# Experts on their chosen rows only: sorted blocks of 128 rows in place of dense experts

## The chip, the cores and the metric

The kernel runs on one core of a Trainium2 chip. Five engines work side by side, each with its own instruction queue in a fixed order: TensorE (PE, matmuls, with PEld for the loading of its weights), VectorE (DVE), ScalarE (ACT), GpSimd (POOL) and SyncE (SP, which mainly issues DMAs). ACT and POOL can issue DMAs too. An instruction that waits holds back all that stand behind it in its engine's queue. The metric is the device time of one execution in microseconds (us), lower is better. All numbers are float32.

## The reference, cut to what matters

x is 16 sequences of 256 tokens with 128 features. Attention has 16 heads of width 8, causal; then a feed-forward part with 8 experts of which each token uses its two best, and two layer norms.

```python
x = _layernorm(x + attention(x))              # w_qkv, rotary positions, causal softmax, w_proj
flat_x = x.reshape(-1, 128)                   # 4096 rows
logits = flat_x @ W_router + b_router         # 8 experts
top_vals, top_idx = top_k(logits, 2)
router_weights = softmax(logits where chosen, -inf elsewhere)
for e in range(8):
    h = relu(flat_x @ W1[e] + b1[e])          # 128 -> 512
    y = h @ W2[e] + b2[e]                     # 512 -> 128
    final_output += y * (router_weights[:, e] * chosen[:, e])[:, None]
x = _layernorm(x + final_output)
```

The weight of an expert that a token did not choose is zero, so only two of the eight products per token count.

## The kernel before

Tokens go in tiles of 128 rows; a sequence has two tiles (NT), a feed-forward block has two sequences (BB), so four tiles or 512 tokens. All weights of all experts are loaded once and stay on the chip (`w1_sb`, `w2_sb`, lines 103 to 107), with DMAs issued by SP.

`attention(b, x1)` is a generator that yields after each step. It transposes the sequence (line 170), makes Q and K (lines 179 and 182, 128x256 matmuls), V (202), and then goes through 12 units. A unit is one bank of scores: `scores` does one matmul with 32 rows of contraction, as four heads of width 8 share a row group (222), DVE adds the causal mask and takes the maximum (230, 232), ACT the exponentials (237); two units later `turn` transposes four 128x128 pieces on PE (246) and copies them back (249 on ACT, 251 on DVE); one unit later `weigh` does eight (four for the first query tile) matmuls with only 9 columns (262). `finish` divides, transposes (279), multiplies by w_proj (284), adds the residual (286) and normalizes: statistics on DVE (146, 147), the root on POOL (149, 150), the result on DVE (152).

`experts(blk, x1)` is a second generator. It transposes the block's 512 rows (314), does the router (321 and small DVE operations) and then all eight experts on all 512 rows: four 128x512 matmuls per expert into `ps_h` (391), relu and bias on ACT (394), sixteen 128x128 matmuls into `ps_y` (401) and on DVE the weighted sum into `acc` (411). Then the second layer norm, and a DMA to the output.

The loop at lines 428 to 448 runs the experts of one block in between the attention steps of the next: for 44 attention steps 39 expert steps are taken. So the attention of the first two sequences runs without expert work beside it, and the experts of the last block without attention. The tile framework then orders each engine's instructions by priority and puts in all waits. It keeps DMAs of the SP and ACT queues on eight semaphores in turn, and a DMA waits until the previous one of its semaphore has landed.

In the trace a float32 matmul appears as two records (x512 for 256 matmuls in line 391), a PE transpose as one.

Of the kernel before, what the change touches and what calls it, by code (L numbers as in the profile page):

```python
# [11 lines left out]
F32 = mybir.dt.float32  # L12
AF = mybir.ActivationFunctionType
ALU = mybir.AluOpType
AX = mybir.AxisListType
PSUM = bass.MemoryType.PSUM

P = 128  # partitions, and the model's width
HEADS = 16
HD = 8  # width of a head  # L20
GROUPS = 4  # row groups of the tensor engine, four heads in each
# [5 lines left out]
def kernel(  # L27
# [16 lines left out]
    nc = tc.nc  # L44

    B, S, D = x.shape
    E, _, FF = w1.shape
    NT = S // P  # token tiles of a sequence
    FC = FF // P
    BB = 2  # sequences of a feed-forward block  # L50
    G = BB * NT  # token tiles of a block
    TB = G * P

# [6 lines left out]
    p4 = ctx.enter_context(tc.tile_pool(name="p4", bufs=4))  # L60
    ps_sc = ctx.enter_context(tc.tile_pool(name="ps_sc", bufs=2, space=PSUM))
# [3 lines left out]
    ps_h = ctx.enter_context(tc.tile_pool(name="ps_h", bufs=2, space=PSUM))  # L65
    ps_y = ctx.enter_context(tc.tile_pool(name="ps_y", bufs=1, space=PSUM))

# [10 lines left out]
    w1_sb = const.tile([P, E, FF], F32, name="w1_sb")  # L78
    w2_sb = const.tile([P, E, FC, D], F32, name="w2_sb")
    b2_sb = const.tile([G * E, G, D], F32, name="b2_sb")  # L80

# [18 lines left out]
    nc.gpsimd.memset(b2_sb, 0.0)  # L100
    for g in range(G):
        nc.sync.dma_start(b2_sb[g * E : (g + 1) * E, g, :], b2)
    for e in range(E):
        nc.sync.dma_start(w1_sb[:, e, :], w1[e])
        nc.sync.dma_start(w2_sb[:, e, :, :], w2[e].rearrange("(c p) d -> p c d", p=P))
        if e + 2 < B:
            load_x(e + 2)
    for b in range(E + 2, B):
        load_x(b)

# [1 line left out]
    ident = const.tile([P, P], F32, name="ident")  # L112
    make_identity(nc, ident)
    # 0 where the key is not after the query, for the diagonal blocks of four heads
# [11 lines left out]
    # E - e, so that of equal logits the first one has the largest  # L126
    rank = const.tile([P, G, E], F32, name="rank")
    for e in range(E):
        nc.gpsimd.memset(rank[:, :, e : e + 1], float(E - e))
    neg_half = const.tile([P, G], F32, name="neg_half")  # L130
    nc.gpsimd.memset(neg_half, -0.5)

    # the weights of Q and K with the halves of each head swapped
# [6 lines left out]

    def normalize(dst, r, n, tag):
        """Rows of r [P, n, D] to mean 0 and variance 1, into dst."""
        mv = p4.tile([P, n, 2], F32, tag=f"mv{tag}", name="mv")
        for t in range(n):
            st = p4.tile([P, 6], F32, tag=f"st{tag}", name="st")
            nc.vector.bn_stats(st, r[:, t, :])
            nc.vector.bn_aggr(mv[:, t, :], st)  # L147
        rstd = p4.tile([P, n], F32, tag=f"rstd{tag}", name="rstd")
        nc.gpsimd.tensor_scalar(rstd, mv[:, :, 1], EPS, None, ALU.add)  # L149
        nc.gpsimd.tensor_tensor(rstd, rstd, neg_half[:, :n], ALU.pow)  # L150
        for t in range(n):
            nc.vector.tensor_scalar(  # L152
                dst[:, t, :],
                r[:, t, :],
                mv[:, t, 0:1],
                rstd[:, t : t + 1],
                ALU.subtract,
                ALU.mult,
            )

# [1 line left out]
    def attention(b, x1):  # L162
# [12 lines left out]
        # Q and K by head on the partitions, turned by their positions  # L175
# [14 lines left out]
        # K four times, each with one head of each row group and zeros elsewhere  # L190
# [6 lines left out]
        # V by token, with a column of ones after each head  # L197
# [14 lines left out]
        # units: (query tile, row group, its heads), one bank of scores each  # L212
# [98 lines left out]
    def experts(blk, x1):  # L311
        psx = ps_misc.tile([P, TB], F32, tag="misc", name="ps_x1T")
        for g in range(G):
            nc.tensor.transpose(psx[:, ts(g, P)], x1[:, g, :], ident)
        x1T = p2.tile([P, TB], F32, tag="x1T", name="x1T")
        nc.scalar.copy(x1T, psx)  # L316
        yield

        psl = ps_misc.tile([P, G, E], F32, tag="misc", name="ps_lg")
        for g in range(G):  # L320
            nc.tensor.matmul(  # L321
                psl[:, g, :], x1T[:, ts(g, P)], wr_sb, start=True, stop=True
            )

        def small(name, last=E):
            return p2.tile([P, G, last], F32, tag=name, name=name)

        def wide(t):
            return t.to_broadcast([P, G, E])

        V = nc.vector
        lg = small("lg")
        for g in range(G):
            V.tensor_tensor(lg[:, g, :], psl[:, g, :], br_sb, ALU.add)

        def first_max(v, tag):
            """The largest of v, and 1 at the first place that has it, 0 elsewhere."""
# [4 lines left out]
            V.tensor_tensor(key, key, rank, ALU.mult)  # L342
# [7 lines left out]
        _, hot2 = first_max(rest, "2")  # L350
        V.tensor_tensor(hot1, hot1, hot2, ALU.add)
        ex = small("ex")
        V.tensor_tensor(ex, lg, wide(m1), ALU.subtract)
        nc.scalar.activation(ex, ex, AF.Exp)
        V.tensor_tensor(ex, ex, hot1, ALU.mult)
        total = small("total", 1)
        V.tensor_reduce(total, ex, AX.X, ALU.add)
        V.reciprocal(total, total)
        wt = small("wt")
        V.tensor_tensor(wt, ex, wide(total), ALU.mult)  # L360
        yield

        acc = p2.tile([P, G, D], F32, tag="acc", name="acc")
        psy = None

        def output_biases():
            """acc = x1 + the experts' second biases, weighted."""
            psw = ps_misc.tile([G * E, P], F32, tag="misc", name="ps_wT")
            nc.tensor.matmul(
                psw, wt.rearrange("p g e -> p (g e)"), ident, start=True, stop=True  # L370
            )
            wT = p2.tile([G * E, P], F32, tag="wT", name="wT")
            nc.scalar.copy(wT, psw)
            yield
            psb = ps_misc.tile([P, G, D], F32, tag="misc", name="ps_b2")
            nc.tensor.matmul(psb, wT, b2_sb, start=True, stop=True)  # L376
            V.tensor_tensor(acc, psb, x1, ALU.add)
            yield

        biases = output_biases()  # L380
        hidden = {}
        for e in range(E + 1):
            if e < E:
                hT = p2.tile([P, FC, TB], F32, tag="hT", name="hT")
                hidden[e] = hT
            if e > 0:
                psy = ps_y.tile([P, G, D], F32, tag="y", name="ps_y")
            for c in range(max(FC, G)):
                if e < E and c < FC:
                    psh = ps_h.tile([P, TB], F32, tag="h", name="ps_h")  # L390
                    nc.tensor.matmul(  # L391
                        psh, w1_sb[:, e, ts(c, P)], x1T, start=True, stop=True
                    )
                    nc.scalar.activation(  # L394
                        hidden[e][:, c, :], psh, AF.Relu, bias=b1_sb[:, e, c : c + 1]
                    )
                if e == 0 and c > 0:
                    next(biases, None)
                if e > 0 and c < G:
                    for f in range(FC):  # L400
                        nc.tensor.matmul(  # L401
                            psy[:, c, :],
                            hidden[e - 1][:, f, ts(c, P)],
                            w2_sb[:, e - 1, f, :],
                            start=(f == 0),
                            stop=(f == FC - 1),
                        )
                yield
            if e > 0:
                for g in range(G):  # L410
                    V.scalar_tensor_tensor(  # L411
                        acc[:, g, :],
                        psy[:, g, :],
                        wt[:, g, e - 1 : e],
                        acc[:, g, :],
# [3 lines left out]
        y = p2.tile([P, G, D], F32, tag="yout", name="yout")  # L419
        normalize(y, acc, G, "f")  # L420
        nc.sync.dma_start(out_t[:, blk * G : (blk + 1) * G, :], y)
        yield
# [3 lines left out]
    ATT_STEPS, FFN_STEPS = 44, 39  # L426
    before = None
    for blk in range(B // BB + 1):
# [78 lines left out]
```

## Time and profile before

| | us |
|---|---|
| median of 3 runs | 1158.97 |
| the runs | 1155.66 to 1171.31 |
| span of the profiled execution | 1160.2 |

The busy time of the main groups, from the page's part 5:

| line | what | busy us | mean ns of a record |
|---|---|---|---|
| 391 | expert matmul 128x512, x512 | 280.4 | 638 |
| 401 | expert matmul 128x128, x2048 | 287.7 | 286 |
| 222 | scores, 32 rows, 512 columns, x384 | 230.6 | 725 |
| 262 | weigh, 9 columns, x1536 | 209.6 | 264 |
| 246 | transposes, x768 | 146.5 | 310 |
| 394 | relu on ACT 128x512, x256 | 176.2 | 688 |

Busy time of PE is a count of the records' extent. A matmul record that lasts longer than the same shape elsewhere is a sign that it ran at another pace, so rows of the same line at two places in the span are worth comparing. The row PEclk of the page shows the granted clock, in tenths of full speed.

### The profile page before, as it was taken

Reading aid. Unit: us, or ns where it says so; the run is one execution under the profiler, and the core shown is the slowest. Engines: PE = TensorE matmul, PEld = TensorE weight load, DVE = VectorE, ACT = ScalarE, POOL = GpSimd, SP = SyncE. Lnnn points to the kernel's source line nnn. Section 1 sums busy time; section 2 is a strip of 40 time slices with the busy share of each in tenths; the row PEclk is TensorE's granted clock in tenths of the full one; section 3 lists DMA queues with packets and bytes.
Section 4 is the critical chain, followed back from the end, with each engine's and each line's share of the span. In section 5 each row is a group of like instructions: output and inputs, shape, how many; then the busy total and the mean of one; then the engine's idle time right before and its main releaser. Section 6 shows DMA issues by size and latency. Waiting matters only on the chain.

```text
span 1160.2 us, 14412 instructions
## 1 busy us (share of the span) xinstructions
PE 1106.2 (95%) x5696; PEld 759.5 (65%) x5696; DVE 523.3 (45%) x1364; ACT 407.8 (35%) x937; POOL 54.4 (5%) x146
## 2 busy tenths in 40 slices
PE   7979899998999999998999989999999989999996
PEld 3656667665676757666676756767566665766675
DVE  4333353546434463445435464344634545344412
ACT  2212143433334244332334433342433324343242
POOL 1000000001000000001000010000000010000000
PEclk9999989999899999999799998999979998899999
DMA  8000000000000000000000000000000000000000
GB/s 231 18 1 0 1 1 1 1 1 10 1 1 1 1 10 1 1 1 10 1 1 1 1 10 1 1 1 1 10 1 1 1 3 8 1 1 2 10 1 10
DMA packets 19202, 10.20 MB, mean 9 GB/s; under 512 B 5280, under 2 KB 17984, under 8 KB 19136
## 3 DMA queue, kind: packets, MB, share of 16 engines
q1 hardware_dynamic: 18560, 8.96, 2.9%
q8 instruction: 45, 0.74, 0.3%
q10 hardware_dynamic: 576, 0.33, 0.1%
q14 instruction: 21, 0.17, 0.0%
HBM read 7.19 MB, written 2.10 MB: 8 GB/s over the span
## 4 chain that ended last, share of the span: by engine, by line
PE 90%; DVE 6%; POOL 2%; ACT 1%; issue 1%; DMA 0%; POOLq 0%; DVEq 0%; ACTq 0%
PE ps_y L401 21%; PE ps_h L391 19%; PE ps_sc L222 19%; PE ps_av L262 15%; PE ps_tr L246 10%; DVE acc L411 1%; PE ps_proj L284 1%; PE ps_qk L182 1%; PE ps_qk L179 1%; DVE parts L184 1%; POOL rstd L150 1%; PE ps_lg L321 1%; DVE yout L152 1%; DVE nmax L232 1%; PE ps_b L376 1%
## 5 line engine op out<-in xcount | busy, mean ns | idle before, releaser
L401 PEld LDWEIGHTS ps_y<-w_sb,hT 128*128 128x128 f32 x2048 | 275.0, 201 | 99.7 <-issue 85.9
L394 ACT ACTIVATE hT<-ps_h,b_sb 128x512 f32<-128x512 f32 x256 | 176.2, 688 | 405.1 <-PE ps_h L391 405.1
L401 PE MATMUL ps_y<-w_sb,hT 128*128 128x128 f32 x2048 | 287.7, 286 | 3.2 <-DVE acc L411 3.2
L391 PE MATMUL ps_h<-x1T,w_sb 128*128 128x512 f32 x512 | 280.4, 638 | 0.0
L222 PE MATMUL ps_sc<-kTm,qk 32*128 32x512 f32 x384 | 230.6, 725 | 0.8 <-DVE kTm L193 0.8
L237 ACT ACTIVATE pr<-ps_sc,nmax 128x256 f32<-128x256 f32 (+1 forms) x512 | 180.3, 420 | 134.5 <-DVE nmax L232 133.8
L230 DVE TENSOR_TENSOR ps_sc<-ps_sc,causal 128x256 f32<-128x256 f32 (+1 forms) x192 | 99.9, 520 | 277.2 <-PE ps_sc L222 276.8
L262 PEld LDWEIGHTS ps_av<-vaug,pT 128*128 128x128 f32 x1536 | 215.7, 217 | 0.0
L262 PE MATMUL ps_av<-vaug,pT 128*128 128x9 f32 x1536 | 209.6, 264 | 0.0
L246 PEld LDWEIGHTS ps_tr<-ident,pr 128*128 128x128 f32 x768 | 97.2, 155 | 138.8 <-issue 103.1
L246 PE MATMUL ps_tr<-ident,pr 128*128 128x128 f32 x768 | 146.5, 310 | 7.3 <-ACT pr L237 6.8
L411 DVE SCALAR_TENSOR_TENSOR acc<-ps_y,wt,acc 128x128 f32<-128x128 f32 x256 | 76.8, 342 | 156.1 <-PE ps_y L401 156.1
L232 DVE TENSOR_REDUCE nmax<-ps_sc 128x2 f32<-128x512 f32 (+1 forms) x192 | 131.9, 687 | 3.0
L251 DVE COPY pT<-ps_tr 128x512 f32<-128x512 f32 x128 | 88.0, 687 | 38.2 <-PE ps_tr L246 38.2
L391 PEld LDWEIGHTS ps_h<-x1T,w_sb 128*128 128x128 f32 x512 | 83.5, 197 | 30.0 <-issue 19.3
L222 PEld LDWEIGHTS ps_sc<-kTm,qk 32*128 32x128 f32 x384 | 58.8, 203 | 49.0 <-issue 30.9
L249 ACT COPY pT<-ps_tr 128x512 f32<-128x512 f32 x64 | 37.5, 586 | 89.2 <-PE ps_tr L246 89.2
L149 POOL TENSOR_SCALAR rstd<-mv 128x1 f32<-128x1 f32 (+1 forms) x40 | 9.8, 244 | 816.2 <-DVE mv L147 816.2
L184 DVE TENSOR_TENSOR parts<-ps_qk,rope_sb 128x512 f32<-128x512 f32 x32 | 21.9, 685 | 34.0 <-PE ps_qk L182 34.0
L179 PE MATMUL ps_qk<-xT,wqkv_sb 128*128 128x256 f32 x64 | 24.1, 461 | 10.4 <-ACT x1T L316 4.7
L272 DVE RECIPROCAL rec<-ps_av 128x16 f32<-128x16 f32 x32 | 8.2, 258 | 50.8 <-PE ps_av L262 50.1
L150 POOL TENSOR_TENSOR rstd<-rstd,neg_half 128x1 f32<-128x1 f32 (+1 forms) x40 | 26.3, 658 | 3.3
(65 smaller groups left out, 347.4 us busy)
## 6 DMA issues: line engine op xcount, KB each, us to landing
w_sb<-in_L_ffn_W_dram SPq DMA_DIRECT2D x16, 256.0 KB, 5.4
x<-in_L_attn_x_dram SPq DMA_DIRECT2D x16, 128.0 KB, 5.0
out_dram<-yout SPq DMA_DIRECT2D x8, 256.0 KB, 2.3
rope_sb<-in_rope_dram SPq DMA_DIRECT2D x1, 512.0 KB
wqkv_sb<-in_L_attn_w_qkv_dram ACTq DMA_DIRECT2D x1, 192.0 KB, 3.0
wproj_sb<-in_L_attn_w_proj_dram ACTq DMA_DIRECT2D x1, 64.0 KB
bproj_sb<-in_L_attn_b_proj_dram ACTq DMA_DIRECT2D x1, 64.0 KB
b_sb<-in_L_ffn_b_dram SPq DMA_DIRECT2D x4, 4.0 KB
```

The costliest lines, as they stand in the source:

```text
L150: nc.gpsimd.tensor_tensor(rstd, rstd, neg_half[:, :n], ALU.pow)
L222: nc.tensor.matmul(ps, qT[rg, ts(qi, P)], kTm[rg, js[0] : js[0] + len(js), 0:nk], start=True, stop=True,)
L230: nc.vector.tensor_tensor(diag, diag, causal[:, : len(js), :], ALU.add)
L232: nc.vector.tensor_reduce(nmax[:, : len(js)], ps, AX.X, ALU.max, negate=True)
L237: nc.scalar.activation(pr[:, n, :], ps[:, n, :], AF.Exp, bias=nmax[:, n : n + 1])
L246: nc.tensor.transpose(ps[:, n, :], pr[:, ts(n, P)], ident)
L251: nc.vector.tensor_copy(pT, ps)
L262: nc.tensor.matmul(av[qi][:, h, 0 : HD + 1], pT[:, n * (qi + 1) + kt, :], vaug[:, kt, h, :], start=(kt == 0), stop=(kt == qi),)
L391: nc.tensor.matmul(psh, w1_sb[:, e, ts(c, P)], x1T, start=True, stop=True)
L394: nc.scalar.activation(hidden[e][:, c, :], psh, AF.Relu, bias=b1_sb[:, e, c : c + 1])
L401: nc.tensor.matmul(psy[:, c, :], hidden[e - 1][:, f, ts(c, P)], w2_sb[:, e - 1, f, :], start=(f == 0), stop=(f == FC - 1),)
L411: V.scalar_tensor_tensor(acc[:, g, :], psy[:, g, :], wt[:, g, e - 1 : e], acc[:, g, :], ALU.mult, ALU.add,)
```

## The change

Attention stays as it is. The feed-forward part is done anew, in two groups of 8 sequences (16 tiles, 2048 tokens each):

- `logits(b)` follows the attention of each sequence: two transposes of the normalized rows, an ACT copy, two 8-column matmuls, two DVE adds.
- `route(g)`, once per group: the two best experts of each token on DVE, counts by two 128x128 matmuls (a triangle of ones and all ones), a running sum, and from it for each token and choice the row (`dest`) in a table in HBM in which rows are sorted by expert, each expert's run filled up to a multiple of 128. `expert` says for each of the 2*16+8-1 = 39 blocks of 128 rows which expert it belongs to. Then 32 indirect DMAs on the POOL queue write the rows (128 rows of 512 B each) into that table.
- `block(g, j)`, 39 times per group: SP reads the expert's number into a register and loads that expert's parameters (128 x 1156 floats, 592 KB, from a packed copy in HBM) and the block's 64 KB of rows; one transpose, four 128x128 matmuls, a DVE maximum with -b1 in place of relu, four 128x128 matmuls, a DVE add of the bias (b2 plus W2 times b1), a store to a second table issued by ACT.
- `combine(g)`: 32 indirect DMAs on the POOL queue fetch each token's two rows, DVE adds them with their weights, then the layer norm and the store.
- At the start: the packed copy is written from HBM to HBM on the SP queue, zeros are written to the row tables (ten DMAs, 5.1 MB) on the ACT queue, `output_bias` makes the joint bias of each expert with five matmuls.
- The order: group 0's attention without expert work beside it; group 1's attention with group 0's blocks in between; then group 1's blocks and combine.

```diff
+    pack = dram.tile([E, P, WROW], F32, name="pack")
...
     for e in range(E):
-        nc.sync.dma_start(w1_sb[:, e, :], w1[e])
-        nc.sync.dma_start(w2_sb[:, e, :, :], w2[e].rearrange("(c p) d -> p c d", p=P))
+        nc.sync.dma_start(pack[e, :, 0:O2], w1[e])
+        nc.sync.dma_start(
+            pack[e, :, O2:OB].rearrange("p (c d) -> p c d", c=FC),
+            w2[e].rearrange("(c p) d -> p c d", p=P),
+        )
...
+    def output_bias(e):
+        w2_sb = p2.tile([P, FC, D], F32, tag="w2", name="w2_sb")
+        nc.scalar.dma_start(w2_sb, w2[e].rearrange("(c p) d -> p c d", p=P))
...
+            nc.tensor.matmul(
+                ps,
+                b1_sb[:, e, c : c + 1].to_broadcast([P, P]),
+                w2_sb[:, c, :],
...
+        nc.scalar.copy(bias, ps)
+        nc.scalar.dma_start(pack[e, :, OB:ON], bias)
...
+    def logits(b):
+        t0 = b * NT
+        psx = ps_misc.tile([P, S], F32, tag="misc", name="ps_x1T")
+        for t in range(NT):
+            nc.tensor.transpose(psx[:, ts(t, P)], x1_sb[:, t0 + t, :], ident)
+        x1T = p2.tile([P, S], F32, tag="x1T", name="x1T")
+        nc.scalar.copy(x1T, psx)
+        yield
...
+    class Routed:
+        def __init__(self, r, b0, n):
+            self.t0, self.T = b0 * NT, n * NT
+            self.NB = 2 * self.T + E - 1
+            self.rows = dram.tile([self.NB * P, D], F32, tag=f"rows{r}", name="rows")
+            self.back = dram.tile([self.NB * P, D], F32, tag=f"back{r}", name="back")
...
+                nc.scalar.dma_start(flat[:, i : i + n], zeros[:, :n])
...
+        for t in range(T):
+            for k in range(2):
+                put = nc.gpsimd.indirect_dma_start(
+                    out=g.rows[:, :],
+                    out_offset=bass.IndirectOffsetOnAxis(
+                        ap=g.dest[:, k, t : t + 1], axis=0
+                    ),
+                    in_=x1_sb[:, t0 + t, :],
...
+    def block(g, j):
+        e = nc.values_load(
+            g.expert[0:1, j : j + 1],
+            engines=[SP],
...
+        w = p3.tile([P, WROW], F32, tag="w", name="w")
+        nc.sync.dma_start(w, pack[bass.ds(e, 1), :, :].rearrange("o p f -> (o p) f"))
+        rows_in = p3.tile([P, D], F32, tag="rows_in", name="rows_in")
+        nc.sync.dma_start(rows_in, g.rows[ts(j, P), :])
+        yield
+        pst = ps_f.tile([P, P], F32, tag="f", name="ps_rT")
+        nc.tensor.transpose(pst, rows_in, ident)
+        rT = p3.tile([P, P], F32, tag="rT", name="rT")
+        nc.scalar.copy(rT, pst)
+        yield
+        psh = ps_f.tile([P, FC, P], F32, tag="f", name="ps_h")
+        for c in range(FC):
+            nc.tensor.matmul(psh[:, c, :], w[:, ts(c, P)], rT, start=True, stop=True)
...
+        V.tensor_tensor(
+            hT,
+            psh,
+            w[:, ON:WROW].rearrange("p (c o) -> p c o", o=1).to_broadcast([P, FC, P]),
+            ALU.max,
+        )
+        yield
+        psy = ps_f.tile([P, D], F32, tag="f", name="ps_y")
+        for c in range(FC):
...
+        V.tensor_tensor(y, psy, w[:, OB:ON], ALU.add)
+        nc.scalar.dma_start(g.back[ts(j, P), :], y)
+        yield
...
+    def combine(g):
...
+                    nc.gpsimd.indirect_dma_start(
+                        out=yk,
+                        out_offset=None,
+                        in_=g.back[:, :],
...
+        if g.t0 == 0:
+            for i, _ in enumerate(attn):
+                if i % (2 * ATT_STEPS // E * 2) == 0:
+                    next(biases, None)
...
+        else:
+            p = groups[0]
+            left = interleave(attn, n * ATT_STEPS, pending, (p.NB - 6) * FFN_STEPS)
+            pending = left
+        for _ in route(g):
+            next(pending, None)
+            next(pending, None)
+        for _ in pending:
+            pass
+        pending = chain(*(block(g, j) for j in range(g.NB)), combine(g))
+    for _ in pending:
+        pass
```

In the instruction order of the built program, PE has no block in the 8 sequences of group 0, six blocks in each of sequences 8 to 13 (in sequence 8 after the scores of its eighth unit), three in sequence 14, none in sequence 15 and 39 after it. POOL has its 32 writes of group 0 before sequence 8's first normalization, and its fetches of group 0 within sequence 15. On ACT the ten stores of zeros, each of which waits for an earlier DMA, stand ahead of the first sequence's copy of V and of all its exponentials. On PE the two transposes of `logits` stand ahead of the next sequence's first transposes.

More of the change, by code (lines that the diff above doesn't have):

```diff
@@ L16 @@
 PSUM = bass.MemoryType.PSUM
+DRAM = bass.MemoryType.DRAM
+SP = mybir.EngineType.SP
 P = 128
@@ L380, in experts @@
[L380 to L392, printed above, removed]
-                    )
[L394 to L410, printed above, removed]
@@ new lines, in route @@
+        m2, hot2 = first_max(rest, "2")
+        hot = small("hot")
+        V.tensor_tensor(hot, hot1, hot2, ALU.add)
+        psc = ps_misc.tile([P, 2, T, E], F32, tag="misc", name="ps_count")
+        nc.tensor.matmul(psc[:, 0], before, hot, start=True, stop=True)
+        nc.tensor.matmul(psc[:, 1], ones, hot, start=True, stop=True)
+        runs = p2.tile([P, E, T + 1], F32, tag="runs", name="runs")
+        V.tensor_copy(runs[:, :, 0:T], psc[:, 1].rearrange("p t e -> p e t"))
+        total = p2.tile([P, E, 1], F32, tag="total", name="total")
@@ new lines, in route @@
+        V.tensor_tensor(ends, ends, runs, ALU.subtract)
+        place = small("place")
+        V.tensor_tensor(
+            place, psc[:, 0], ends[:, :, 0:T].rearrange("p e t -> p t e"), ALU.add
+        )
+        for k, h in enumerate((hot1, hot2)):
+            V.tensor_tensor(h, h, place, ALU.mult)
+            with nc.allow_low_precision(reason="whole numbers"):
+                V.tensor_reduce(
+                    g.dest[:, k, :].rearrange("p (t o) -> p t o", o=1), h, AX.X, ALU.add
+                )
@@ L418, in experts @@
                     )
[L419 to L428, printed above, removed]
[L429 to L448 removed]
+                yield
```

255 lines of the change are left out of this document (174 added, 81 removed).

## Prediction, made before the changed kernel ran

> **What bounds the kernel now.** I read the page first: busy times and slices.
>
> ```profile
> PE 1106.2 (95%) x5696; PEld 759.5 (65%) x5696; DVE 523.3 (45%) x1364; ACT 407.8 (35%) x937; POOL 54.4 (5%) x146
> PE   7979899998999999998999989999999989999996
> PEclk9999989999899999999799998999979998899999
> ```
>
> PE is busy all the time, and lines 391 and 401, the experts, hold 568 of its 1106 us. That invites the sum "a quarter of the expert work, so 380 us less". Before believing it I cut the span into stretches: sequence 0 from its first scores to those of sequence 1, a steady block, and the last block's experts alone (columns: length, then busy us and count of PE, PEld, DVE, ACT, POOL, granted clock, DMA share, GB/s).
>
> ```profile
> 12.50:77.90 65.40, 59.31 (x188) 39.84 (x188) 25.36 (x52) 14.58 (x42) 2.60 (x7) 1.00 0.30 85
> 431.60:565.10 133.50, 129.47 (x713) 88.85 (x712) 65.17 (x170) 50.64 (x117) 6.53 (x16) 0.97 0.01 3
> 1092.00:1150.00 58.00, 56.78 (x310) 39.27 (x310) 13.24 (x57) 22.25 (x34) 1.27 (x2) 1.00 0.02 5
> ```
>
> One sequence of attention without expert work takes 65.4 us. Two sequences together with a whole block of experts take 133.5 us. So the experts cost almost nothing where they run beside attention, though alone they need some 64 us of PE per block. The rows of single lines say why: the second sequence (77.9 to 134) against a steady stretch (585 to 695), then PE's timeline at one of the places where expert rows are sparse (start, extent in us).
>
> ```profile
> L222 PE MATMUL ps_sc<-kTm,qk x24: 1056/1136/1217, 77.9 to 119.1; 32*128 32x512 f32 x24
> L222 PE MATMUL ps_sc<-kTm,qk x36: 587/640/692, 588.8 to 694.1; 32*128 32x512 f32 x36
> L246 PE MATMUL ps_tr<-ident,pr x48: 421/421/476, 82.0 to 128.5; 128*128 128x128 f32 x48
> L246 PE MATMUL ps_tr<-ident,pr x72: 272/273/330, 584.7 to 693.4; 128*128 128x128 f32 x72
> ...
> 558.39 0.94 PE L401 MATMUL ps_y<-w_sb,hT 128*128 128x128 f32 x6
> ...
> 562.03 0.96 PE L262 MATMUL ps_av<-vaug,pT 128*128 128x9 f32 x8
> 562.84 0.47 PE L401 MATMUL ps_y<-w_sb,hT 128*128 128x128 f32 x2
> 563.24 2.01 PE L222 MATMUL ps_sc<-kTm,qk 32*128 32x512 f32 x2
> 565.18 1.12 PE L246 MATMUL ps_tr<-ident,pr 128*128 128x128 f32 x4
> 566.09 1.72 PE L262 MATMUL ps_av<-vaug,pT 128*128 128x9 f32 x8
> 567.65 2.05 PE L391 MATMUL ps_h<-x1T,w_sb 128*128 128x512 f32 x2
> ```
>
> Same instructions, same shapes, but PE runs at half pace whenever it has only attention: 32-row scores, transposes and 9-column matmuls. Medians go from 640 to 1136 ns and from 273 to 421 ns. The pace falls at 563.2, after about 4 us with only 0.4 us of expert rows, and returns at 581.1, after expert rows had filled 7.9 of some 13 us. Such a dip recurs every 133 us, where expert rows are sparse. The granted clock reads 1.00 in the slow stretch, so that column hides it; the durations decide. The Trainium skill ("TensorE: Matmul & The Clock Gate", Part 1) states a gate that opens after about 3.4 us of sustained matmul activity and falls back after an idle window; taken as a rule on PE's idle gaps it would keep these sequences fast, for PE is 90% busy there. The rows say no: busy with such small matmuls is not enough.
>
> So before is attention at a pace that the dense experts keep up. The change takes three quarters of them away, and for half the sequences all.
>
> **The change part by part.** Slow, a record of line 401's shape takes 0.23 us of PE (ps_v in the slow stretch, 0.93 us of weight loads for 4), fast 0.127 us (30.54 us for 240 in the last stretch).
>
> *Start.* On ACT the ten stores of zeros stand before the copy of V, and each waits for an earlier DMA. By the queue order some 9.8 MB must land before the last is issued; the loads of before ran at 305 to 337 GB/s in 15 to 30 us, and at 180 over the first 40 us. That is 31 to 54 us against some 12 us where V is copied now: **25** us, 10 to 55. All of attention stands behind it.
>
> *Sequences 0 to 7, no expert beside them.* 65.4 us each. Behind each, `logits` now waits for the norm before the next sequence may use PE and the one misc bank: at 134.50 the residual add starts and at 136.96 the normalized rows are there (2.5 us), then transposes 0.7, copy 0.4, matmuls 0.5, adds 0.2, hand-overs 0.3, less 0.4 that the next sequence waits today: 4.2, taken as 4.5. The eight output biases are 10 records x 0.23 = 2.3 us each. 8 x 69.9 + 18 = **577** us.
>
> *Route of group 0.* Some 26 small DVE operations at 0.2 to 0.3 us stand before sequence 8's on DVE: **8** us. Its 32 indirect writes hold POOL, where sequence 8's norm and, behind that on DVE, its last units wait. No row shows an indirect DMA. From below: POOL's smallest real operation, 0.57 us (line 150). From above: 3.0 us, issue to landing of one 192 KB load. Nearer to the lower end, as eight may be in flight: 1.3 us, so 42 us; sequence 8 needs over 50 us to come to that norm, so nothing here (at 2.5 us: 30).
>
> *Sequences 8 to 14 with 39 blocks.* A block is a transpose and 8 matmuls, 16 records: slow 0.25 + 16 x 0.23 = 3.9 us, fast 2.2 us. A sequence is 69.9 us slow; fast it is (133.5 - 64)/2 = 34, plus 2.5 for `logits`. All slow: 7 x 69.9 + 39 x 3.9 = 641 us. All fast: 256 + 86 = 342 us. Which? Six blocks in a sequence of 92 us are 23 us of expert rows, a quarter, against half in a steady block now. They are uneven: at the sequence boundary blocks stand beside Q, K and V, about as dense as at 142 to 145 us, where the fast pace began; in the ten middle units there are 0 to 4 short matmuls per unit, as sparse as before 563. So fast for a third: 641 - 299/3 = **541** us.
>
> *Sequence 15.* Alone again, 69.9; group 0's fetches and sums on POOL and DVE stand among its own: **80** us.
>
> *The tail.* Routing 10 us, 32 writes x 1.3 = 42, with PE idle, landing and first load 3. Then 39 blocks in a chain that nothing fills: transpose 0.33, copy 0.27 (line 281), four matmuls 1.2, maximum 0.69 (the 128x512 of line 377), four matmuls 1.2, hand-overs 0.3: 3.9 us fast, 5.8 slow. Expert rows fill over half of it, as much as a steady block now, so fast: 152 us. Parameters, rows and result are 720 KB per block, 185 GB/s at that pace, below the 305 seen, and three buffers prefetch: hidden; SP's register reads too, unless they take over 3 us. Then landing 3, 32 fetches x 1.3 = 42, last norm and store 6 (1153.0 to the end today is 7). Together **258** us, 200 to 440 with 0.57 to 3.0 us per indirect DMA and both paces. By the skill's fit for GpSimd's DMAs ("DMA: Bandwidth & Descriptors", Anatomy of one DMA: 2.0 us plus bytes over 436 GB/s) a write of 64 KB alone would take 2.15 us; were they one after another, the tail would be 54 us longer, an estimate that no row here tests.
>
> What goes: 568 us of PE, 176 of ACT (394), 77 of DVE (411). It is gained only where PE was the limit by it, and it was the limit in 8 blocks of 133 us, two sequences each.
>
> Sum: 25 + 577 + 8 + 541 + 80 + 258 = 1489, say **1490** us, against 1160 of the profiled execution, which stands within 0.1% of the median, so no correction.
>
> **The rivals.**
> *The slow pace belongs to the start, not to missing experts* (faster). Then all attention runs at 34 + 2.5 us: 25 + 8 x 36.5 + 18 + 8 + 342 + 37 + 258 = 980 us. It decides if sequences 2 to 7 show transposes of 273 ns. For it: only two sequences without experts are to be seen, and loads ran in the first 30 us. Against it: the second sequence, with 0 to 1 GB/s, is as slow, and each dip falls where expert rows are sparse. 4%.
> *The thin blocks keep the pace* in sequences 8 to 14: 1489 - 199 = 1290 us. For it: once fast, stretches with under a third of expert rows stayed fast; against it: the dips. 13%.
> *Slow throughout and dear indirect DMAs*: 641 in sequences 8 to 14, 5.8 us per block in the tail (+74), 2.2 us per indirect DMA (+57 in the tail): 1720 us. For it: a quarter of expert rows is little, and the chain leaves gaps. 25%.
> *Blocks take more than one expert's work*: the number of blocks is fixed, 39 for 32 tiles' worth of rows, and is in the sum; that something else is computed, 2%.
>
> **How the numbers follow.** The forecast's own case, 1400 to 1600, has 56%. 1340 to 1700 leaves out the faster case, most of the fast-pace one and a third of the dear one, some 2 in 10. Within 2% is about what a measurement of this kernel can tell from no change; only a mixture with nearly everything fast gets there. Faster 0.04, same 0.02, slower 0.94.
>
> **What would show it.** Right: transposes of about 421 ns and 70 us per sequence in 0 to 7 and 15; both paces in 8 to 14; a tail of over 200 us in which PE is idle during the indirect DMAs. Wrong: transposes of 273 ns in sequences 1 to 7; blocks in the tail of more than 6 us (then loads or SP's register reads bound it); a start later than 60 us.

## The result and the profile after

| | before | after |
|---|---|---|
| median, us | 1165.14 (4 runs, 1155.66 to 1177.12) | 1477.07 (4 runs, 1474.41 to 1488.14) |
| span of the profiled execution, us | 1160.2 | 1476.0 |
| ratio of the times, 95% interval | | 1.270 (1.260 to 1.281) |

The change makes the kernel 27% slower. The runs before are the three of the first table and a fourth of 1177.12 us. From the page of the changed kernel, the busy times and two rows of the 40 slices:

```profile
PE 1160.6 (79%) x4518; PEld 826.6 (56%) x4518; DVE 531.1 (36%) x1246; ACT 262.4 (18%) x761; POOL 190.0 (13%) x294
PE   3697979888898979679999999999998780366620
PEclk8555555555555555557766666566655555699975
```

PE has fewer records than before (4518 against 5696) and is busy for longer (1160.6 against 1106.2 us). Fewer and longer records point to another pace, not to more work. The stretches of the span show where (columns: length, then busy us and count of PE, PEld, DVE, ACT, POOL, granted clock, DMA share, GB/s). In order they are sequences 1 to 7, sequences 8 to 14 with 39 blocks, sequence 15, the routing and writes of group 1, its 39 blocks, and its fetches:

```profile
121.40:610.60 489.20, 428.99 (x1358) 287.97 (x1358) 179.12 (x378) 104.38 (x294) 17.93 (x49) 0.50 0.00 0
619.50:1139.50 520.00, 486.29 (x2022) 355.72 (x2022) 213.26 (x466) 113.99 (x333) 55.93 (x85) 0.64 0.20 60
1139.50:1213.00 73.50, 61.69 (x189) 40.50 (x189) 36.28 (x107) 14.72 (x41) 32.47 (x39) 0.50 0.13 33
1213.00:1271.00 58.00, 2.72 (x9) 2.04 (x9) 11.59 (x54) 0.59 (x2) 34.11 (x38) 0.50 0.22 74
1271.00:1417.00 146.00, 97.79 (x663) 80.53 (x663) 38.21 (x78) 10.34 (x39) 0.00 (x0) 0.97 0.63 181
1417.00:1476.00 59.00, 0.00 (x0) 0.00 (x0) 19.30 (x81) 0.00 (x0) 40.72 (x48) 0.53 0.21 55
```

Seven sequences without blocks take 69.9 us each, at a clock of 0.50. In the two stretches around the last blocks, 117 us, PE does next to nothing. The rows of the transposes (line 246 is line 299 now) and of the scores (222 is 275), in sequences 2 to 6 and, for the transposes, in the second stretch, say the same without the clock column:

```profile
L299 PE MATMUL ps_tr<-ident,pr x240: 420/422/477, 203.8 to 530.0; 128*128 128x128 f32 x120
L275 PE MATMUL ps_sc<-kTm,qk x120: 1052/1136/1218, 199.7 to 520.6; 32*128 32x512 f32 x120
L299 PE MATMUL ps_tr<-ident,pr x336: 272/421/476, 632.2 to 1127.4; 128*128 128x128 f32 x168
```

The three figures are minimum, median and maximum in ns. The first row has no record at the fast pace (minimum 420 ns). The last has both, and its median is the slow one. The end of the writes and the first block, from the chain of waits (start, length, what):

```profile
1266.07 0.98 POOL rows L488
1267.04 0.30 issue
1267.35 0.98 POOL rows L488
1268.33 0.30 issue
1268.63 2.24 DMA rows<-x_sb,dest
1270.87 0.02 issue
1270.89 1.74 DMA rows_in<-rows
1272.63 0.04 issue
1272.67 0.49 PE ps_rT L517
```

An indirect write takes 0.98 us of POOL and 0.30 us until the next, 1.28 us in all, and PE waits for the last of 32.

### The profile page after: what moved, and what is told of

It is laid out like the page before. It is cut to its first block, busy times and chain, and to the rows that moved or that the text cites. A ratio compares the mean times of both kernels' runs of the same rounds, so it can differ in the third digit from the quotient of the medians.

```text
span 1476.0 us, 13114 instructions
## 1 busy us (share of the span) xinstructions
PE 1160.6 (79%) x4518; PEld 826.6 (56%) x4518; DVE 531.1 (36%) x1246; ACT 262.4 (18%) x761; POOL 190.0 (13%) x294
## 4 chain that ended last, share of the span: by engine, by line
PE 71%; DVE 9%; POOL 8%; issue 5%; DMA 3%; ACT 2%; SPq 0%; POOLq 0%; ACTq 0%; DVEq 0%
PE ps_sc L275 21%; PE ps_av L315 17%; PE ps_tr L299 12%; PE ps_h L523 6%; PE ps_y L537 6%; POOL rows L488 4%; POOL yk L559 2%; DVE hT L528 2%; PE ps_qk L232 2%; DMA pack<-in_L_ffn_W_dram 1%; PE ps_qk L235 1%; PE ps_proj L337 1%; POOL rstd L203 1%; DVE parts L237 1%; DVE nmax L285 1%
## 5 line engine op out<-in xcount | busy, mean ns | idle before, releaser
L315 PEld LDWEIGHTS ps_av<-vaug,pT 128*128 128x128 f32 x1536 | 336.4, 322 | 0.2 <-issue 0.2
L275 PE MATMUL ps_sc<-kTm,qk 32*128 32x512 f32 x384 | 330.6, 1065 | 7.0 <-DVE kTm L246 7.0
L315 PE MATMUL ps_av<-vaug,pT 128*128 128x9 f32 x1536 | 316.5, 337 | 0.0
L299 PE MATMUL ps_tr<-ident,pr 128*128 128x128 f32 x768 | 212.6, 425 | 48.5 <-ACT pr L290 46.9
L537 PE MATMUL ps_y<-w,hT 128*128 128x128 f32 x624 | 108.5, 317 | 34.1 <-DVE hT L528 34.1
L523 PE MATMUL ps_h<-rT,w 128*128 128x128 f32 x624 | 107.7, 317 | 18.3 <-ACT rT L519 18.3
L537 PEld LDWEIGHTS ps_y<-w,hT 128*128 128x128 f32 x624 | 90.5, 217 | 50.0 <-DVE hT L528 48.1
L523 PEld LDWEIGHTS ps_h<-rT,w 128*128 128x128 f32 x624 | 91.1, 220 | 32.5 <-ACT rT L519 31.0
L559 POOL DMA_INDIRECT yk<-back,dest x64 | 66.2, 1034 | 197.0 <-DMA back<-y 165.1
L488 POOL DMA_INDIRECT rows<-x_sb,dest x64 | 62.8, 982 | 39.3 <-DVE dest L472 20.4
```

The lines of the kernel that those rows point to most:

```text
L275: nc.tensor.matmul(ps, qT[rg, ts(qi, P)], kTm[rg, js[0] : js[0] + len(js), 0:nk], start=True, stop=True,)
L299: nc.tensor.transpose(ps[:, n, :], pr[:, ts(n, P)], ident)
L315: nc.tensor.matmul(av[qi][:, h, 0 : HD + 1], pT[:, n * (qi + 1) + kt, :], vaug[:, kt, h, :], start=(kt == 0), stop=(kt == qi),)
L488: put = nc.gpsimd.indirect_dma_start(out=g.rows[:, :], out_offset=bass.IndirectOffsetOnAxis(ap=g.dest[:, k, t : t + 1], axis=0), in_=x1_sb ...
L523: nc.tensor.matmul(psh[:, c, :], w[:, ts(c, P)], rT, start=True, stop=True)
L537: nc.tensor.matmul(psy, hT[:, c, :], w[:, O2 + c * D : O2 + (c + 1) * D], start=(c == 0), stop=(c == FC - 1),)
```

## The experiments

Theory: PE's pace depends on how much of its array works. Attention alone (32-row scores, 9-column products, transposes) leaves it at half pace; the dense experts kept it up, so they cost almost nothing, and taking them away gains almost nothing. Rivals: the pace has to do with the place in the program, or with gaps in PE's work, whatever the products; or the attention is slow by its own waits.

**The attention alone.** The kernel before without lines 391, 394, 401 and 411.

```diff
-                    nc.tensor.matmul(psh, w1_sb[:, e, ts(c, P)], x1T, start=True, stop=True)
-                    nc.scalar.activation(hidden[e][:, c, :], psh, AF.Relu, ...)
...
-                            nc.tensor.matmul(psy[:, c, :], hidden[e - 1][:, f, ts(c, P)], ...)
...
-                    V.scalar_tensor_tensor(acc[:, g, :], psy[:, g, :], wt[:, g, e - 1 : e], ...)
```

> The kernel before with the experts left out: their two products, the relu and the weighted sum into the accumulator are not computed (router, biases' part and both norms stay), so its time is that of the attention and what stands round it. Mine: the experts' products in the kernel before paid for themselves by the pace; without them all 16 sequences run at the slow pace, 16 x 65 to 69 us + 35 to start and 15 to end = 1090 to 1150 us, hardly less than 1159. Rival (the experts cost what PE spends on them, about 64 us of each pair's 133): 1159 - 8 x 64 = 650 us.

Measured: 1106.78 us, span 1104.8, ratio to before 0.944 (0.941 to 0.947). The transposes of this run (minimum, median and maximum in ns, over the whole span):

```profile
L246 PE MATMUL ps_tr<-ident,pr x768: 417/421/477, 16.6 to 1078.4; 128*128 128x128 f32 x192
```

Not one of 768 ran at the fast pace. The dense experts, 568 us of PE by their records, cost 1160.2 - 1104.8 = 55 us by the profiled spans. The runs of the kernel before lie between 1156 and 1178 us and these two at 1107, so by single runs it is 49 to 71 us. Leaving them out altogether gains no more; so little was there for cheaper experts to win, unless they lifted the pace of the attention too. (This run keeps the router, the biases' part and both norms.)

**Full-size products among the attention.** One and then two products per unit step, in the sequences that have no blocks; then two that contract over 32 rows.

```diff
+    def filler(k, kTm):
+        for _ in range(k):
+            ps = ps_f.tile([P, 4 * P], F32, tag="f", name="ps_fill")
+            nc.tensor.matmul(ps, wqkv_sb[:, 0, :],
+                kTm[:, 0:2, :].rearrange("p j s -> p (j s)"), start=True, stop=True)
...
+        fill = 1 if b < 8 or b == 15 else 0      # second run: 2
...
                 scores(i)
+            filler(fill, kTm)
```

```diff
-            nc.tensor.matmul(ps, wqkv_sb[:, 0, :],
-                kTm[:, 0:2, :].rearrange(...), ...)
+            nc.tensor.matmul(ps, wqkv_sb[0:32, 0, :],      # third run
+                kTm[0:32, 0:2, :].rearrange(...), ...)
```

> The changed kernel, with one more matrix product (128 x 512 by 128 x 128, result unread) at each of the 15 unit steps of sequences 0 to 7 and 15, the ones without expert blocks. Nothing else differs, and the output is computed as before. Mine (a lone sequence is slow because its products use 32 rows or 9 columns and leave PE at half pace; full-size products among them bring the full pace): the 70 us of such a sequence become 36 (its PE work at the fast pace) + 15 x 0.9 = 50, so nine of them give about 1477 - 180 = 1297 us, with transposes of 273 ns in them in place of 421. If the mechanism holds but one product per step is too thin, the pace stays and each adds 1.8 to 2 us: about 1477 + 9 x 28 = 1730 us. Rival (the pace does not depend on what the products are, only on the place in the program or on PE's share of time): also about 1730 us, with transposes of 421 ns; the second run of this set separates the two.

> As the run before, with two such products at each of the 15 steps, 30 in a sequence. Mine: the full pace in sequences 0 to 7 and 15, each 36 + 30 x 0.9 = 64 us, in all 1477 - 9 x 6 = about 1420 us, although 270 full-size products were added. Rival (the pace has nothing to do with full-size products): each costs 1.8 to 2 us at the slow pace, 70 + 57 = 127 us a sequence, about 1990 us.

> As the run before, with the added products contracted over 32 rows only (the same 512 columns and 128 outputs, so the same time on PE). Mine (what lifts the pace is work on all 128 rows): the pace stays half in sequences 0 to 7 and 15, each added product costs 1 us or more there, between 1477 + 9 x 30 = 1750 and 1990 us. Rival (any work that closes PE's gaps lifts it): as in the run before, about 1420 us, with transposes of 273 ns.

Measured: 1454.79, 1559.71 and 1836.60 us. The transposes and the added products in sequences 2 to 5, which have no blocks, and the whole of sequence 4, two products per step on all rows:

```profile
L311 PE MATMUL ps_tr<-ident,pr x192: 272/273/273, 216.3 to 494.7; 128*128 128x128 f32 x192
L218 PE MATMUL ps_fill<-kTm,wqkv_sb x240: 592/592/1222, 206.3 to 497.0; 128*128 128x512 f32 x120
349.20:425.90 76.70, 70.59 (x254) 37.65 (x254) 26.58 (x54) 15.26 (x42) 2.57 (x7) 0.86 0.00 1
```

The same on 32 rows:

```profile
L311 PE MATMUL ps_tr<-ident,pr x192: 421/421/475, 260.3 to 659.3; 128*128 128x128 f32 x192
L218 PE MATMUL ps_fill<-kTm,wqkv_sb x240: 1056/1056/1217, 248.1 to 663.9; 32*128 32x512 f32 x120
```

Same count, same columns, and the place in PE's queue is the same. With all rows every transpose in these sequences is fast, and a sequence takes 76 us with 30 added products, PE being busy for 92% of it; a slow stretch is left at its start, ahead of the first transposes (clock 0.86). With 32 rows none is fast, and it takes 109, with PE busy for 95%. That is the theory's side in both, and the rival that any work which fills PE's gaps lifts the pace falls. The third time lies in its expected range; the first two are 158 and 140 us above the theory's, though below the rival's. I had taken an added product at 0.9 us, and its two records are 592 ns each, so 30 cost 35 us and not 27. With one product per step the pace rises in the units and falls again at the boundaries of sequences, where no products were added, and in sequences 2 and 6 in the middle too: 62.7 and 60.5 us in the better sequences, 66.9 in the mean of 1 to 6 against 69.9. And sequence 15 with the tail took 369 and 395 us, against 337 in the changed kernel: there blocks and fetches of group 0 slid behind the attention. Its last fetch starts at 1210 us in the changed kernel, before the last logits, and with two products per step 104 us behind them. So filling buys little: it pays for the pace with PE time.

**The same scores on all rows.** The number of score products, their columns and results stay; the keys are masked per head in place of per four heads, so all 128 rows can be contracted.

```diff
-                qT[rg, ts(qi, P)],
-                kTm[rg, js[0] : js[0] + len(js), 0:nk],
+                qT[:, ts(qi, P)],
+                kTh[g][:, js[0] : js[0] + len(js), 0:nk],
...
+        def mask(g):
+            kTh[g] = p2.tile([P, 4, S], F32, tag=f"kTh{g}", name="kTh")
+            for j in range(4):
+                h = 4 * g + j
+                nc.vector.tensor_scalar(kTh[g][:, j, :], kT, own_sb[:, h : h + 1], None, ALU.mult)
```

> The changed kernel with another form of the score products only: the keys are masked for each of 16 heads (16 DVE multiplications of 0.35 us a sequence in place of 4), and each score product contracts over all 128 rows in place of 32. The number of products, their columns and their result are the same, and no work is added on PE. Mine (the pace hangs on how many rows of the array work): the full pace in the attention, a lone sequence of 45 to 52 us in place of 70, a score product of about 640 ns in place of 1065; with 16 x 20 us less, 1110 to 1200 us in all. Rival (the pace is half because of the transposes, the 9-column products or the gaps, whatever the rows of the scores): as before plus up to 4 us of DVE a sequence, 1477 to 1540 us.

Measured: 1212.61 us (ratio to before 1.035, 1.026 to 1.044), 264 us below the changed kernel, although DVE has 192 more multiplications. The transposes and scores of sequences 1 to 7 in this run:

```profile
L326 PE MATMUL ps_tr<-ident,pr x336: 272/273/475, 106.3 to 468.3; 128*128 128x128 f32 x168
L300 PE MATMUL ps_sc<-kTh,qk x168: 592/676/1222, 102.1 to 461.0; 128*128 128x512 f32 x168
```

Medians of 273 and 676 ns, against 422 and 1136 in the changed kernel. Maxima of 475 and 1222 say that slow stretches remain: most stand at the boundaries of sequences, and sequences 1, 4, 5 and 6 have one of 10 to 14 us in the middle. So a lone sequence takes 55.5 us in the mean of 1 to 6 and not 45 to 52, and the total is 13 us above the range expected. This is the run that settles the cause: no product was added on PE, and there only the number of working rows differs, in the score products and in the loads of their weights.

**The same edit on the kernel before, and on its attention alone.**

> The kernel before with the scores contracted over all 128 rows (keys masked for each of 16 heads), its dense experts and all else as they were. Mine (before, the experts keep the full pace but for the first 145 us and some 8 dips of 4 to 16 us): only these are left to win, 20 to 50 us, about 1110 to 1140 us; so the same edit that took 264 us from the changed kernel takes a fifth of that here. Rival (the edit helps by itself, through the score products and not through the pace): 16 x 16 us as in the changed kernel, about 900 us.

> The kernel before without the experts' products, relu and weighted sum (their part of the output is not computed), as in the run of the attention alone, but with the scores contracted over all 128 rows. Mine: the 65 to 70 us of a sequence become 46 to 52, in all 16 x 49 + 45 = 780 to 880 us against 1107; the difference of that to the kernel before with the same edit is then what the experts cost when they no longer pay for the pace. Rival (the attention is slow by its own waits): 1050 to 1107 us.

Measured: 1054.14 us (ratio 0.903, 0.895 to 0.911), and 822.30 us. The attention alone gains 287 us, as expected. The kernel before gains 106 us by the spans, more than twice what I expected of it, less than half of the rival's. A pair of sequences, before and then with the edit:

```profile
203.60:336.90 133.30, 129.26 (x715) 88.88 (x713) 65.18 (x170) 50.65 (x117) 6.49 (x17) 0.97 0.01 3
```

```profile
169.90:293.20 123.30, 119.68 (x715) 87.98 (x713) 69.73 (x194) 51.12 (x117) 6.54 (x17) 1.00 0.01 3
```

The same 715 PE records take 9.6 us less: the slow stretches in a pair cost 10 us and not the 2 to 8 that I had read from the dips. Six pairs, which gain 7 to 14 us each, the last pair with the end of the kernel, 14 us, and a start that is 28 us shorter (sequence 2 begins at 106.9 in place of 134.8) make the gain.

With this pair of runs the loss can be taken apart. From the starts of the sequences in the profiled executions comes each part's excess, the time it takes in the changed kernel less the time it takes in the attention alone: first as the kernels stand, then with the scores on 128 rows in both.

| part | excess, us | excess with 128-row scores, us |
|---|---|---|
| up to the start of sequence 1 | 51.9 | 42.2 |
| sequences 1 to 7 and route of group 0 | 25.7 | 46.1 |
| sequence 8 | 10.3 | 29.3 |
| sequences 9 to 14 with their blocks | 32.2 | 5.9 |
| sequence 15 and the tail | 251.0 | 269.0 |
| sum: routed experts | 371.2 | 392.5 |
| dense experts in their place | 55.4 | 236.8 |
| loss by the change | 315.8 | 155.7 |

In the left column the routed experts cost 371 us and the dense ones 55: that is the whole loss. In the right column the attention no longer needs the dense experts for its pace, and they cost 237; the loss halves, but the change still loses. What is left is not the blocks beside attention, for six sequences with 33 blocks cost 6 us (partly because the blocks lift the pace further: clock 0.94 in that stretch, 0.79 without blocks). It is the serial parts: start, logits and routing, tail.

**The parts around the attention.** The stores of zeros moved to SP's queue:

```diff
-                nc.scalar.dma_start(flat[:, i : i + n], zeros[:, :n])
+                nc.sync.dma_start(flat[:, i : i + n], zeros[:, :n])
```

> The changed kernel with the ten stores of zeros into the row buffers issued on SP, behind the writes of the packed parameters, in place of on ACT ahead of sequence 0. Mine (sequence 0 is late because ACT's queue holds 5 MB of zeros before the loads of W2 that the output biases wait for): 25 to 35 us earlier at the start and the rest as it was, about 1445 us. Rival (the bytes fill the 16 DMA engines whatever queue they come from): sequence 1 still starts at 121 us, about 1477 us.

Measured: 1457.27 us, 20 us less. From PE's timeline of this run (start, length; idle time before it in brackets):

```profile
96.59 0.69 PE L223 MATMUL ps_xT<-ident,x 128*128 128x128 f32 x2 [0.33 <-DVE lg_sb L378]
```

In the changed kernel this same line starts at 121.36. The same bytes were stored, so it is their place ahead of ACT's work, and not their volume, that made 25 us of the late start.

Five groups of 2, 4, 4, 4 and 2 sequences, with this move:

```diff
-    ROUTED = [8, 8]
+    ROUTED = [2, 4, 4, 4, 2]
...
-            p = groups[0]
-            left = interleave(attn, n * ATT_STEPS, pending, (p.NB - 6) * FFN_STEPS)
-            pending = left
+            p = groups[groups.index(g) - 1]
+            steps = p.NB * FFN_STEPS + 3 * (p.T // NT)
+            pending = interleave(attn, n * ATT_STEPS, pending, steps)
```

> The changed kernel with five groups of 2, 4, 4, 4 and 2 sequences in place of two of 8 (99 blocks in place of 78; the blocks of a group still run in the next one's attention), and the stores of zeros on SP. Mine: the last group leaves 15 blocks behind the attention in place of 39, so the tail falls from 263 to about 95 us; three more routings cost 3 x 9 us; a sequence with blocks stays at 71 to 75 us: about 1330 to 1360 us. Rival (what is taken from the tail comes back in the sequences that now carry 84 blocks in place of 39): within 40 us of 1477.

Measured: 1422.16 us, so the rival was nearer than the theory. PE's timeline at the end of sequence 15 and at the first block after it:

```profile
1304.93 0.47 PE L368 MATMUL ps_x1T<-ident,x_sb 128*128 128x128 f32 x1 [25.31 <-DVE x_sb L205]
...
1330.65 0.47 PE L517 MATMUL ps_rT<-ident,rows_in 128*128 128x128 f32 x1 [18.03 <-DMA rows_in<-rows]
```

The tail did shrink, from 263 to 111 us (1304.93 to 1416.1). But the start of sequence 15, 25 us earlier by the zeros, came 81 us later: 106 us went into sequences that carry 84 blocks and into three more routings, mostly at the slow pace (clock 0.66 from sequence 2 to 14), and PE stood 25.31 us before the last logits, because the norm's POOL operations waited behind fetches.

**Everything together.** Five groups, scores on 128 rows, zeros on SP, and each sequence's logits within the next sequence's attention (at unit steps 4 and 8). A second version also put the routing into the next group's attention; a third ran a group's fetches after the next group's routing and ahead of its blocks.

```diff
-    def attention(b, x1):
+    def attention(b, x1, before_it):        # the logits of sequence b - 1
...
+            if i in (4, 8):
+                next(before_it, None)
```

```diff
-        for _ in route(g):
-            next(pending, None)
-            next(pending, None)
...
-        pending = chain(*(block(g, j) for j in range(g.NB)), combine(g))
+        pending = chain(logits(first_b + n - 1), route(g),      # second version
+            *(block(g, j) for j in range(g.NB)), combine(g))
...
+        pending = chain(early, older, blocks)                   # third: logits and route, the group before's combine, blocks
```

> The five groups, the scores over 128 rows, the zeros on SP, and each sequence's logits computed within the next sequence's attention in place of between the two. Mine (each of the four takes its own part): 45 us to start, two sequences of 47 us, fourteen with 6 blocks each of about 58, four routings of 9, tail 95 us: about 1050 to 1090 us, below the kernel before. Rival (the half pace stays, whatever the rows): 1270 to 1340 us.

> The version of the last set (five groups, scores over 128 rows, zeros on SP, logits within the next attention) with the routing of a group and its last logits also within the next group's attention, and the rows put and fetched by POOL spread out, so that the norm's two POOL operations at the end of a sequence no longer wait behind fetches (13.9 us of idle PE ahead of one set of logits). Mine: three group boundaries of some 25 us less, about 985 to 1020 us. Rival (the boundaries' idle time returns as waits of the first blocks for their rows): 1050 to 1074 us.

> The last version again, with what its trace showed idle taken out: a group's fetches and weighted sums run after the next group's routing and before its blocks, so that the blocks no longer wait for their rows (6.6 us of idle PE at one boundary) and the last group's rows are put before the fetches of the group ahead of it (45 us at the tail, 925 to 970 us); and a fetch is issued five steps ahead of the sum that reads it. Mine: 35 to 45 us off the tail and 5 to 10 at each of four boundaries, about 985 to 1010 us, below the kernel before and its version with scores over 128 rows (1054). Rival (these waits return elsewhere): 1045 to 1065 us.

| version | median, us | ratio to before, 95% |
|---|---|---|
| first | 1074.17 | 0.918 (0.911 to 0.925) |
| second | 1064.28 | 0.911 (0.901 to 0.920) |
| third | 1050.29 | 0.907 (0.896 to 0.918) |
| dense experts, scores on 128 rows | 1054.14 | 0.903 (0.895 to 0.911) |

Every run of the four (1042 to 1078 us) lies below every run of the kernel before. The first hit its expectation in the total, partly by luck: sequences 2 to 15 with four routings took 819 us where 848 were expected, and the tail 121 where 95 were. The two after it hardly gained, and their rivals held. In the third, the last pair of sequences with what follows:

```profile
767.00:859.00 92.00, 58.21 (x283) 42.30 (x282) 47.47 (x149) 16.11 (x47) 39.18 (x48) 0.68 0.25 76
859.00:922.00 63.00, 61.20 (x441) 51.07 (x439) 40.69 (x93) 19.51 (x57) 0.82 (x3) 1.00 0.57 165
922.00:1041.00 119.00, 53.00 (x341) 44.13 (x341) 39.97 (x137) 5.63 (x21) 38.86 (x46) 0.78 0.45 134
```

The first sequence of the pair carries the routing and 39 us of POOL, takes 92 us and falls to a clock of 0.68; the second, full of blocks, keeps 1.00 with PE at 97%. Against the second version the time from the first transpose of the last logits on is 13 us shorter (117 against 130), and 10 of these came back in this pair. Routed experts beat the kernel before, by 9%, but so does the edit of the scores alone with the dense experts, and these runs show no difference between the two.

## Why the prediction was right

1490 us were predicted and 1477 measured. The terms, by the profiled spans (the start is 121.4 us to sequence 1, less 69.4 of the attention alone, less 4.5 for `logits`):

| term | predicted | measured |
|---|---|---|
| start and output biases | 25 + 18 | 47 |
| a sequence without blocks | 69.9 | 69.9 |
| route of group 0 | 8 | 8.9 |
| sequences 8 to 14 with 39 blocks | 541 | 520 |
| sequence 15 | 80 | 73.5 |
| tail | 258 | 263 |

No term is far off. That the sum is within 1% owes a little to luck: sequences 8 to 15 were 27 us cheaper than forecast, the start, the routing and the tail 10 us dearer.

*The pace.* The step that carried the forecast was that sequences 0 to 7 run as the second sequence of the kernel before did, at half pace. They do, and the runs show why: full-size products or 128-row scores bring the fast pace, 32-row products of the same length do not. The rival that the pace belongs to the start falls with the attention alone, slow over its 1105 us. The Trainium skill ("TensorE: Matmul & The Clock Gate", Part 1) describes the gate by how busy PE is in a window of some 3.4 us; here PE was busy for 103.40 of 109.30 us in a sequence with 32-row products added, and slow throughout. So being busy did not suffice here, and the number of rows at work decided.

*Sequences 8 to 14.* "Fast for a third" was near: a clock of 0.64 between 0.50 and 1.00 is 28%. The fast stretches lie at the boundaries of sequences (680 to 718, 761 to 783 and so on), the slow ones in the middle units. With 28% the forecast's own bounds give 641 - 0.28 x 299 = 557 us, and 520 were measured: a block beside attention was priced too high, by about 1 us each (37 us over 39 blocks, an estimate). So the rival in which thin blocks keep the pace falls, and so does the dear one, slow throughout.

*Indirect DMAs.* 1.3 us were taken between 0.57 and 3.0 us. The writes follow each other every 1.28 to 1.30 us, the last fetches every 1.3 to 1.44 us and every 2.0 with a norm's two operations between. By the Trainium skill's fit ("DMA: Bandwidth & Descriptors", Anatomy of one DMA) 64 KB alone would take 2.15 us, an estimate; the last write landed 2.24 us after its start on POOL. So the fit is near for the landing of one, while a row of them overlaps and costs 1.28 us each.

*The tail.* Its terms were off in both directions: logits and routing 15.7 us and not 10, landing and first load 4.0 and not 3, the blocks 3.7 us each and not 3.9, the end from 1417 on 59 and not 51, because the norms of eight sequences stand between the fetches on POOL. The zeros on ACT were named as what delays the start, with bounds of 10 to 55 us; moving them takes 25 us from it, the value taken, though only 20 from the total.

*What the prediction did not say* is the bound itself: that the experts' whole net cost was 55 us. It had the numbers for a guess, 8 x (133.5 - 2 x 65.4) and the 58.0 us of the last block, about 80 us, and used them for the pace alone.

What stays open: whether the columns in use count as the rows do (the 9-column products were left as they are); whether transposes count as products do (those of line 246 work on all 128 rows and are 218 of 983 us of PE in the attention alone, which was slow all the same); why the pace still falls with 128-row scores, mostly at the boundaries, by idle PE or by the products there; and why the first sequence of each group takes 13 to 31 us more than the others of its group in the second and third routed versions. None of this was tried.

## What to carry to other kernels

Before taking work away, measure what it costs where it stands: leave it out in one run, and compare with its busy time. Here 568 us of PE were worth about 55. And look at one instruction at two places of the span: if it is a third shorter or more beside large matmuls, the small ones set the pace, and giving them the whole array (zeros in unused rows) can be worth more than removing work: it took 106 us from the kernel before and 264 from the changed one with one and the same edit.

## What the runs showed of the hardware that was not expected

In these runs the granted clock did not tell of the slow pace until it had changed once. The row of a sequence with added 32-row products:

```profile
350.60:459.90 109.30, 103.40 (x264) 59.01 (x264) 26.58 (x54) 15.49 (x43) 2.56 (x7) 1.00 0.00 1
```

It reads 1.00 in a stretch whose transposes took 421 ns, and the attention alone reads 1.00 over its whole span. In the changed kernel the same pace reads 0.50. Its mean differed between executions of equal time, too: 0.607 at a span of 1476.0 us and 0.827 at 1474.8. The Trainium skill ("TensorE: Matmul & The Clock Gate", Part 1) warns that the gate's recorded events can be unreliable; the durations of one shape went with the length of the sequences in every run shown here.

The rows shown have two paces: transposes took 272 to 273 or 421 to 422 ns in the median, scores 640 to 676 or 1136. So a record grows by 1.5 to 1.8 times, while the clock, where it tells, goes from 1.00 to 0.50. A change takes place from one group of instructions to the next. PE's timeline at the head of the tail of the changed kernel, where eight records of one shape go from 2.08 and 2.02 to 1.16 us:

```profile
1276.36 2.08 PE L537 MATMUL ps_y<-w,hT 128*128 128x128 f32 x8 [0.78 <-DVE hT L528]
1278.23 0.42 PE L517 MATMUL ps_rT<-ident,rows_in 128*128 128x128 f32 x1
1279.01 2.02 PE L523 MATMUL ps_h<-rT,w 128*128 128x128 f32 x8 [0.35 <-ACT rT L519]
1281.81 1.16 PE L537 MATMUL ps_y<-w,hT 128*128 128x128 f32 x8 [0.78 <-DVE hT L528]
```
